# A hand-over between two stages: the first rows loaded early, the next segment's stores held, sixteen banks first

## The chip, the cores and the metric

The kernel runs on one core of a Trainium2 chip. The metric is the device time of one launch in microseconds (us). Three runs of the kernel before gave 1132.73, 1129.9 and 1131.68; their median, 1131.68, is the time before.

## What is computed

The input `x` has 64 batches of 128 channels and 2048 time steps, all in float32. Two residual layers follow each other:

```python
W = weights[condition]                       # one 128x128 matrix per batch
x = x + einsum('bct,bcd->bdt', x, W)         # layer 0
K = 2 * real(sum_n Ct[h,n] * exp(dtA[h,n] * l))   # a 2048-tap filter per channel, 64 modes
y = irfft(rfft(x, 2L) * rfft(K, 2L))[:L] + x * D  # causal convolution per channel
x = x + y * (t < length[b])                  # layer 1
```

Layer 0 mixes the channels of one batch; layer 1 filters along time within one channel, for all batches. The kernel never takes a transform: it does the convolution in blocks of 128 steps (a Toeplitz matrix inside a block, a recurrence of 64 modes from block to block).

## The kernel before, in words

Time is cut into two segments of 1024 steps (s = 0 and 1).

**The batch stage.** Layer 0 works batch by batch. `fetch(s, n)` loads two batches (1 MB) from `x` on the SP queue into a tile `xb`; `weigh` picks the batch's 128x128 matrix on GpSimd; `project` multiplies it on TensorE in banks of 512 columns, copies each bank back into `xb`, mostly on ScalarE (ACT), and stores the finished batch (512 KB) to a scratch tensor `scr[s]` in DRAM, by a transfer issued on the ACT queue. All 64 batches of segment 0 are done in this stage (`batch0`), while the filter's tables are made between them.

**The group stage.** Layer 1 works by groups of four channels. `load(i)` brings group i back from `scr` with the batches (and two halves of the segment) as 128 partitions: a tile `x` of 128 rows x 2048, 1 MB. There are 32 groups per segment, 64 iterations in all. In `iteration(i)`, for each of four channels n: `turn(i + 1, n)` transposes the next group's channel on TensorE (tile `tr`, line 831) and ACT copies it (`u`, line 832); `inputs` multiplies it (`v`, line 856) and ACT scales the product into `s` (line 861); `inside` multiplies the present group by its Toeplitz blocks (`y`, line 897); and `some` does a few banks of segment 1's layer 0 (`p`, line 459). Then VectorE runs the recurrence (`scan`), TensorE adds its part (line 909), and `store` writes the output.

**Who does segment 1's layer 0.** Its 128 banks (64 batches, two banks each) are spread over the first 28 iterations. `FILL` banks are done up front: before, `some(8)` ahead of the first iteration and 4 within it (i = -1, which only prepares group 0); the other 116 are dealt over iterations 0 to 27, so that four of these take 5 banks and the rest 4.

**What sets the order.** The order is written by hand: each engine runs its instructions in the order in which the Python code calls them. `xb` and `x` tiles share ten buffers in rotation, so a load waits until the tile ten allocations before it is stored. Transfers issued on the SP and ACT queues share eight completion semaphores, dealt out in turn over both queues; an instruction that issues a transfer first waits until the transfer that had its semaphore before has landed, and everything behind it on its engine waits with it. Within PSUM, `p` (after the batch stage), `tr` and the table tile `pb` share two buffers, so a bank or a transpose waits for ACT's copy of the one before last.

Group 0 needs rows of all 64 batches: `load(0)` is issued after the batch stage and waits for the store of batch 63.

Of the kernel before, what the change touches and what calls it, by code (L numbers as in the profile page):

```python
# [41 lines left out]
F32 = mybir.dt.float32  # L42
# [6 lines left out]
P = 128  # L49
# [322 lines left out]
def cond_resid_ssm_kernel(  # L372
# [13 lines left out]
    nc = tc.nc  # L386
    ctx.enter_context(tc.manual_schedule())
    B, C, L = x.shape
# [4 lines left out]
    HL = SL // 2  # L393
# [5 lines left out]
    NG = NP // GP  # L399
    CG = 2 * GP  # L400
# [11 lines left out]
    big = ctx.enter_context(tc.tile_pool(name="big", bufs=10))  # L412
# [4 lines left out]
    scr = [dram.tile([P, C, HL], F32, tag=f"scr{s}", name=f"scr{s}") for s in range(NS)]  # L417
# [17 lines left out]
    def fetch(s, n):  # L435

        xbs[s, n] = big.tile([P, BT, SL], F32, tag="x", name=f"xb_{s}_{n}")
        src = x[n * BT : (n + 1) * BT, :, s * SL : (s + 1) * SL]
        nc.sync.dma_start(xbs[s, n], src.rearrange("b c t -> c b t"))

    def weigh(s, b):

        w1s[s, b] = s0.tile([P, C], F32, tag="w1", name=f"w1_{s}_{b}")
        at = nc.values_load(
            ci[:, b : b + 1],
            engines=(mybir.EngineType.Pool,),
            min_val=0,
            max_val=S - 1,
            skip_runtime_bounds_check_because="it is clamped above",
        )  # L450
        nc.gpsimd.tensor_copy(w1s[s, b], wres[:, bass.ds(at, 1), :].rearrange("p s d -> p (s d)"))  # L451

    def project(s, b, q, ps, n_banks=1, copy=nc.scalar.copy):

        n, r = divmod(b, BT)
        own = xbs[s, n][:, r, :]
        for k in range(n_banks):
            cols = slice((q + k) * BK, (q + k + 1) * BK)
            nc.tensor.matmul(ps[:, k], w1s[s, b], own[:, cols], start=True, stop=True)  # L459
        cols = slice(q * BK, (q + n_banks) * BK)  # L460
        copy(own[:, cols], ps.rearrange("p k t -> p (k t)"))  # L461
        if q + n_banks == QB:
            to = scr[s].rearrange("(f b) c t -> b c f t", f=2)[b]
            nc.scalar.dma_start(to, own.rearrange("c (f t) -> c f t", f=2))
            del w1s[s, b]
            if r == BT - 1:
                del xbs[s, n]

    def batch0(b, copy=nc.scalar.copy):
        if b % BT == 0 and b // BT + AHEAD < B // BT:  # L470
            fetch(0, b // BT + AHEAD)
        if b + WAHEAD < B:
            weigh(0, b + WAHEAD)
        project(0, b, 0, psp.tile([P, QB, BK], F32, tag="y", name=f"p0_0_{b}", bufs=2), QB, copy)
# [7 lines left out]
    def exps(g):  # L482

        for i in range(TP):
            nc.scalar.activation(es[g][:, i, 0, :], steps, AF.Exp, scale=par_of(DRE, g, i))  # L485
# [137 lines left out]
    def partial_angles(k):  # L623

        own = parts[:, :, 0:NL]
        by_l = some_l.unsqueeze(1).to_broadcast([P, NP, NL])

        def of(row, n):
            return gtab[:, row, :].unsqueeze(2).to_broadcast([P, NP, n])

        if k == 0:
            V.tensor_tensor(own, of(FHI, NL), by_l, ALU.mult)
        elif k == 1:
            V.tensor_scalar(whole, own, MAGIC, MAGIC, ALU.add, ALU.subtract)
        elif k == 2:
            V.tensor_tensor(own, own, whole, ALU.subtract)
        elif k == 3:
            V.tensor_tensor(whole, of(FLO, NL), by_l, ALU.mult)
        elif k == 4:
            V.tensor_tensor(own, own, whole, ALU.add)  # L640
        else:
            V.tensor_tensor(parts[:, :, 0:8], parts[:, :, 0:8], of(PHI, 8), ALU.add)
            V.tensor_tensor(parts[:, :, 24:25], parts[:, :, 24:25], of(PHI, 1), ALU.add)
            V.tensor_scalar(last, parts[:, :, 24:25], MAGIC, MAGIC, ALU.add, ALU.subtract)
            V.tensor_tensor(last, parts[:, :, 24:25], last, ALU.subtract)
            V.tensor_scalar(dcol, dcol, 1.0, None, ALU.add)
# [66 lines left out]

    SPAN = 28
    pieces = [(s, b, q) for s in range(1, NS) for b in range(B) for q in range(QB)]
    FILL = 12
    begun = told = done = 0

    def due(i):

        return min(len(pieces), FILL + (len(pieces) - FILL) * (i + 1) // SPAN)

    def some(n):
        nonlocal done
        for s, b, q in pieces[done : done + n]:
            weights_for(done + WAHEAD * QB + 1)
            project(s, b, q, psp.tile([P, 1, BK], F32, tag="tr", name=f"p0_{s}_{b}_{q}", bufs=2))
            done += 1

    def fetches(n):  # L730

        nonlocal begun
        while begun < min(n + BT * QB, len(pieces)):
            fetch(pieces[begun][0], pieces[begun][1] // BT)
            begun += BT * QB

    def weights_for(n):
        nonlocal told
        while told < min(n, len(pieces)):
            weigh(*pieces[told][:2])  # L740
            told += QB

# [14 lines left out]
    for now in range(12, B):  # L759
        batch0(now, V.tensor_copy if now < 18 else nc.scalar.copy)  # L760
        if now == 12:
            with nc.allow_non_contiguous_dma(reason="128 gains, four times"):
                for i in range(TP):
                    nc.gpsimd.dma_start(dcol[i * NR : (i + 1) * NR, :], dbyrow.rearrange("(h r) -> r h", r=NR))
        if now < FIRST:
            partial_angles(now - 12)
        if now < 18:
            exps(2 * now - 20)
            exps(2 * now - 19)
        for lag, step in STEPS.items():  # L770
            g, odd = divmod(now - FIRST - lag, 2)
            if not odd and 0 <= g < NT:
                step(g)
        if now == 60:
            fetches(FILL)
    assert not ps and not ts and not ks
    tmp.__exit__(None, None, None)
    early.__exit__(None, None, None)


    s1 = ctx.enter_context(tc.tile_pool(name="s1", bufs=2))
    xs, us, ss, bts, tts, ys = {}, {}, {}, {}, {}, {}
    half = [slice(0, B), slice(B, P)]
    NI = NS * NG

    def seg(i):
        return divmod(i, NG)

    def load(i):
        s, g = seg(i)  # L790
        xs[i] = big.tile([P, CG, HL], F32, tag="x", name=f"x_{i}")
        nc.sync.dma_start(xs[i], scr[s][:, g * CG : (g + 1) * CG, :])

    def toeplitz(i):

# [5 lines left out]
    def input_weights(i):  # L801

        s, g = seg(i)
        bts[i] = s1.tile([P, GP, 4, N], F32, tag="bt", name=f"bt_{i}")
        if s > 0:
            nc.sync.dma_start(bts[i].rearrange("p d k m -> p (d k m)"), btd[g])
            return
        pb = psp.tile([P, GP, 4, N], F32, tag="tr", name=f"pb_{i}", bufs=2)
        for d in range(GP):
            pair = g * GP + d  # L810
            for part in range(2):
                to = pb[:, d, part : 4 - part : 3 - 2 * part, :]
                nc.tensor.transpose(to, es[pair // TP][:, pair % TP, part, 1:NE], ident)  # L813
        nc.scalar.copy(bts[i], pb)  # L814
# [117 lines left out]
    def iteration(i):  # L932

        nxt = i + 1 < NI
        if i + 2 < NI and seg(i + 2)[0] > 0:
            input_weights(i + 2)
        if i + 3 < NI:
            load(i + 3)
        fetches(due(i + 1))
        if nxt:  # L940
            toeplitz(i + 1)
            if seg(i + 1)[0] == 0:
                input_weights(i + 1)
            states(i + 1)
        quota = due(i) - done
        for n in range(CG):
            if nxt:
                turn(i + 1, n)
            if nxt and n > 0:
                inputs(i + 1, n - 1)  # L950
            if i >= 0:
                inside(i, n)
            some(quota * (n + 1) // CG - quota * n // CG)
        if i > 0:
            store(i - 1)
        if i >= 0:
            carry_on(i)
        if nxt:
            inputs(i + 1, CG - 1)
            keep_weights(i + 1)  # L960
            scan(i + 1, 0, 2 if seg(i + 1)[0] == 0 else 1)
        for d in range(GP):
            if i >= 0:
                outputs(i, d)
            if not nxt:
                store(i, d)
            if nxt and d == 0:
                scan(i + 1, 2, 3) if seg(i + 1)[0] == 0 else scan(i + 1, 1, 2)
        if nxt:
            scan(i + 1, 3 if seg(i + 1)[0] == 0 else 2, NQ)  # L970
    load(0)
    load(1)
    some(8)
    for i in range(-1, NI):
        iteration(i)

# [31 lines left out]
```

## Time and profile before

| What | us |
|---|---|
| median of 3 runs | 1131.68 |
| the profiled execution's own time | 1130.9 |
| span of that execution's trace | 1129.1 |
| TensorE busy in the span | 1078.6 |
| batch stage: last batch copied, at | 186.59 |
| first transpose of group 0, at | 200.45 |
| one iteration with 4 banks / with 5 banks | 16.56 / 17.41 |

All times within an execution count from the start of the span. A busy TensorE says that it had matmuls in flight. "Granted clock" is the share of full speed that TensorE's throttle allowed. The DMA share is the mean busy share of the core's 16 DMA engines.

### The profile page before, as it was taken

What the parts mean: (1) busy time and instruction counts of PE and PEld (TensorE: products, weight loads), DVE (VectorE), ACT (ScalarE), POOL (GpSimd) and SP (SyncE); (2) the same over time, 40 slices, a digit from 0 to 9 for tenths busy, and PEclk for the clock granted to TensorE, in tenths of its full rate; (3) what the DMA queues carried; (4) which work ended last, traced back from release to release, by engine and by line L of the source; (5) the groups of instructions that cost most, each with busy time, mean ns of one, the idle gap of its engine ahead of it and who ended that gap; (6) DMA issues with size and microseconds to landing.
All of it is one profiled execution on the core that took longest, in us unless ns stands there. A gap on an engine that the chain in (4) does not pass through costs nothing.

```text
span 1129.1 us, 23838 instructions
## 1 busy us (share of the span) xinstructions
PE 1078.6 (96%) x8634; PEld 787.5 (70%) x8634; DVE 802.5 (71%) x2671; ACT 680.1 (60%) x1123; POOL 232.5 (21%) x404
## 2 busy tenths in 40 slices
PE   5579998899999999999999999999999999999996
PEld 2224443477777777777767768888888888888885
DVE  7555660376676676667567658888888888888887
ACT  2567665656765666665666566566566556556652
POOL 2112432112212222221221211221111121121110
PEclk9889999899999999999999999999999999999999
DMA  9999999979999999999999887787777788777764
GB/s 276 414 395 369 398 411 389 396 234 309 312 293 302 281 299 309 298 281 300 310 267 297 272 242 225 239 220 217 230 233 224 216 239 228 209 243 226 214 165 117
DMA packets 117462, 313.25 MB, mean 277 GB/s; under 512 B 12002, under 2 KB 12386, under 8 KB 109154
## 3 DMA queue, kind: packets, MB, share of 16 engines
q1 hardware_dynamic: 70928, 218.65, 61.8%
q10 hardware_dynamic: 35986, 67.84, 16.1%
q0 software_dynamic: 10432, 25.25, 8.9%
q8 instruction: 68, 1.11, 0.4%
q14 instruction: 48, 0.39, 0.1%
HBM read 164.76 MB, written 146.93 MB: 276 GB/s over the span
## 4 chain that ended last, share of the span: by engine, by line
PE 90%; DVE 3%; DMA 3%; ACT 2%; issue 1%; ACTq 0%; POOLq 0%; SPq 0%; DVEq 0%; POOL 0%
PE y L909 21%; PE y L897 20%; PE v L856 18%; PE p L459 17%; PE tr L831 10%; DMA scr<-xb 2%; PE pb L813 2%; PE pt L662 1%; PE pk L692 1%; ACT xb L461 1%; DMA x<-scr 1%; DVE s L871 1%; ACT e L485 0%; DVE xb L461 0%; DVE x L918 0%
## 5 line engine op out<-in xcount | busy, mean ns | idle before, releaser
L871 DVE SCALAR_TENSOR_TENSOR s<-s,ptab 128x128 f32<-128x128 f32 x1792 | 521.4, 346 | 110.7 <-ACT s L861 94.9
L861 ACT ACTIVATE s<-v,ptab 64x512 f32<-64x512 f32 (+1 forms) x512 | 335.6, 655 | 50.8 <-PE v L856 33.9
L897 PEld LDWEIGHTS y<-tt,u 128*128 128x128 f32 x2048 | 263.6, 192 | 80.4 <-issue 66.9
L459 PE MATMUL p<-xb,w 128*128 128x512 f32 x512 | 259.1, 619 | 28.5 <-POOL w L451 13.0
L897 PE MATMUL y<-tt,u 128*128 128x128 f32 x2048 | 270.1, 275 | 0.1
L909 PEld LDWEIGHTS y<-e,s 64*128 64x128 f32 x4096 | 233.9, 188 | 46.5 <-issue 24.1
L856 PE MATMUL v<-u,bt 128*128 128x512 f32 (+1 forms) x512 | 248.6, 567 | 0.0
L909 PE MATMUL y<-e,s 64*128 64x128 f32 x4096 | 246.7, 275 | 1.4 <-DVE s L871 1.4
L832 ACT COPY u<-tr 128x512 f32<-128x512 f32 x256 | 150.4, 588 | 158.4 <-PE tr L831 131.8
L880 DVE TENSOR_SCALAR s<-s 128x128 f32<-128x128 f32 x448 | 100.4, 224 | 137.9 <-ACT s L861 137.9
L461 ACT COPY xb<-p 128x512 f32<-128x512 f32 (+1 forms) x186 | 133.2, 717 | 88.9 <-PE p L459 80.3
L918 DVE COPY_PREDICATED x<-mask,y 128x1024 f32<-128x1024 uint8 x128 | 166.7, 1303 | 1.0 <-PE y L909 1.0
L831 PE MATMUL tr<-ident,x 128*128 128x128 f32 x1024 | 156.5, 276 | 5.5 <-DMA x<-scr 5.5
L831 PEld LDWEIGHTS tr<-ident,x 128*128 128x128 f32 x1024 | 121.8, 142 | 56.4 <-issue 50.9
L459 PEld LDWEIGHTS p<-xb,w 128*128 128x128 f32 x512 | 88.2, 199 | 96.5 <-issue 69.3
L451 POOL COPY w<-wres 128x128 f32 x128 | 59.0, 462 | 315.6 <-PE p L459 305.0
L799 POOL DMA_DIRECT2D tt<-kpad x64 | 50.1, 783 | 208.9 <-DVE s L871 173.3
L856 PEld LDWEIGHTS v<-u,bt 128*128 128x128 f32 x512 | 79.9, 192 | 13.8 <-issue 13.6
L844 POOL DMA_DIRECT2D s<-carry x64 | 45.1, 709 | 128.0 <-PE y L909 118.6
L814 ACT COPY bt<-pb 128x512 f32<-128x512 f32 x32 | 18.7, 586 | 87.3 <-PE pb L813 86.5
L888 POOL DMA_DIRECT2D carry<-s x64 | 43.6, 727 | 65.9 <-DVE s L871 60.8
L841 POOL MEMSET s<- 128x384 f32 x32 | 14.5, 454 | 148.3 <-DMA carry<-s 74.2
(193 smaller groups left out, 288.5 us busy)
## 6 DMA issues: line engine op xcount, KB each, us to landing
xb<-in_x_dram SPq DMA_DIRECT2D x64, 1024.0 KB, 9.8
scr<-xb ACTq DMA_DIRECT2D x128, 512.0 KB, 8.5
x<-scr SPq DMA_DIRECT2D x64, 1024.0 KB, 8.0
out_dram<-x SPq DMA_DIRECT2D x126, 512.0 KB, 5.7
tt<-kpad POOLq DMA_DIRECT2D x64, 256.0 KB, 5.6
btd<-bt SPq DMA_DIRECT2D x32, 256.0 KB, 7.3
bt<-btd SPq DMA_DIRECT2D x32, 256.0 KB, 4.9
carry<-s POOLq DMA_DIRECT2D x64, 64.0 KB, 7.0
```

The lines of the kernel that those rows point to most:

```text
L451: nc.gpsimd.tensor_copy(w1s[s, b], wres[:, bass.ds(at, 1), :].rearrange("p s d -> p (s d)"))
L459: nc.tensor.matmul(ps[:, k], w1s[s, b], own[:, cols], start=True, stop=True)
L461: copy(own[:, cols], ps.rearrange("p k t -> p (k t)"))
L831: nc.tensor.transpose(tr[:, k, :], xs[i][:, c, k * Q : (k + 1) * Q], ident)
L832: nc.scalar.copy(u, tr)
L856: nc.tensor.matmul(v[:, 0:nv], w, us[i, n].rearrange("p k r -> p (k r)")[:, 0:nv], start=True, stop=True)
L861: nc.scalar.activation(own[:, 0:nv], v[lanes, 0:nv], AF.Copy, scale=amp)
L871: nc.vector.scalar_tensor_tensor(new[:, d, 0:2], src, factor, own[:, d, 0:2], ALU.mult, ALU.add)
L880: nc.vector.tensor_scalar(old[:, :, 2], old[:, :, 0], -1.0, None, ALU.mult)
L897: nc.tensor.matmul(y[:, k, :], u[:, k, :], tts[i][:, n, :], start=(k == 0), stop=False, skip_group_check=True)
L909: nc.tensor.matmul(ys[i, d][:, c, k, :], st[half[c], d, part, k, :, :].rearrange("p f b -> p (f b)"), e[half[c], pair % TP, part, 0:Q], st ...
L918: nc.vector.copy_predicated(xs[i][:, d::2, :].rearrange("r c (k t) -> r c k t", k=KK), keep_k.unsqueeze(1).to_broadcast([P, 2, KK, Q]), ys ...
```

## The change

It has three parts, all at the seam between the stages:

1. `FILL` goes from 12 to 16: twelve banks of segment 1 run ahead of the first iteration (`some(FILL - CG)`, with `CG` = 4) and four within it. The other 112 are then 4 in each of 28 iterations. A fifth `xb` tile of segment 1 is fetched before group 0 is loaded, because `fetches` covers `FILL` banks and one tile more.
2. `load(0)` is cut by batches: after batch 62's instructions, rows of batches 0 to 55 are loaded in two transfers (one per half of the segment, 56 rows each); after the batch stage, the rows of batches 56 to 63 in two more (8 rows each).
3. Stores of segment 1's batches go through a list `held`. In the batch stage (s = 0) a batch is stored at once, as before. From then on `release` is called once for each n of an iteration: in iteration -1 it issues one held store per call, afterwards all that are held.

```diff
+    held = []
+
+    def release(n=None):
+        for s, b, own in held[:n]:
+            to = scr[s].rearrange("(f b) c t -> b c f t", f=2)[b]
+            nc.scalar.dma_start(to, own.rearrange("c (f t) -> c f t", f=2))
+        del held[:n]
...
         if q + n_banks == QB:
-            to = scr[s].rearrange("(f b) c t -> b c f t", f=2)[b]
-            nc.scalar.dma_start(to, own.rearrange("c (f t) -> c f t", f=2))
+            held.append((s, b, own))
+            if s == 0:
+                release()
...
-    FILL = 12
+    FILL = 16
...
+    EARLY = 56
...
+    def load(i, b0=0, b1=B):
+
+        s, g = seg(i)
+        if b0 == 0:
+            xs[i] = big.tile([P, CG, HL], F32, tag="x", name=f"x_{i}")
+        own = scr[s][:, g * CG : (g + 1) * CG, :]
+        if b1 - b0 == B:
+            nc.sync.dma_start(xs[i], own)
+        else:
+            for f in (0, B):
+                nc.sync.dma_start(xs[i][f + b0 : f + b1], own[f + b0 : f + b1])
...
-        if now == 60:
+        if now == 59:
             fetches(FILL)
+        if now == 62:
+            load(0, 0, EARLY)
...
             some(quota * (n + 1) // CG - quota * n // CG)
+            release(None if i >= 0 else 1)
...
-    load(0)
+    load(0, EARLY, B)
     load(1)
-    some(8)
+    some(FILL - CG)
```

More of the change, by code (lines that the diff above doesn't have):

```diff
@@ L741, in weights_for, with seg @@
             told += QB
+    EARLY = 56
+    xs = {}
+    def seg(i):
+        return divmod(i, NG)
+    def load(i, b0=0, b1=B):
[8 more added lines that the diff above has]
+                nc.sync.dma_start(xs[i][f + b0 : f + b1], own[f + b0 : f + b1])
     ps = {}
@@ L781, in cond_resid_ssm_kernel @@
     s1 = ctx.enter_context(tc.tile_pool(name="s1", bufs=2))
-    xs, us, ss, bts, tts, ys = {}, {}, {}, {}, {}, {}
+    us, ss, bts, tts, ys = {}, {}, {}, {}, {}
     half = [slice(0, B), slice(B, P)]
     NI = NS * NG
[L786 to L792, printed above, removed]
     def toeplitz(i):
```

## The prediction

> **What bounds the kernel now.** I read the page first, then the chain of waits around the seam, then TensorE's timeline and the table of stretches there.
>
> ```profile
> PE 1078.6 (96%) x8634; PEld 787.5 (70%) x8634; DVE 802.5 (71%) x2671; ACT 680.1 (60%) x1123; POOL 232.5 (21%) x404
> PE   5579998899999999999999999999999999999996
> DMA  9999999979999999999999887787777788777764
> ```
>
> TensorE is the bound from the sixth slice on; only the first 200 us, where the DMA engines are full, have slack to give. The chain shows the seam (start, us, what):
>
> ```profile
> 186.59 1.02 ACT xb L461
> 187.62 0.02 issue
> 187.64 5.66 DMA scr<-xb
> ...
> 193.57 6.75 DMA x<-scr
> 200.32 0.14 issue
> 200.45 1.09 PE tr L831 x4
> ```
>
> Batch 63 is copied, its store lands, only then group 0's load starts, and TensorE waits for that:
>
> ```profile
> 188.77 5.70 PE L459 MATMUL p<-xb,w 128*128 128x512 f32 x12 [0.50 <-POOL w L451]
> 194.31 0.64 PE L813 MATMUL pb<-ident,e 128*128 128x128 f32 x4
> 200.45 1.09 PE L831 MATMUL tr<-ident,x 128*128 128x128 f32 x4 [5.50 <-DMA x<-scr]
> ```
>
> ```profile
> 184.00:187.00 3.00, 3.00 (x8) 1.33 (x8) 0.00 (x0) 1.59 (x3) 0.59 (x2) 1.00 1.05 404
> 196.00:199.00 3.00, 0.00 (x0) 0.00 (x0) 0.00 (x0) 0.40 (x1) 0.00 (x0) 0.70 0.98 371
> 199.00:202.00 3.00, 1.55 (x5) 1.25 (x6) 0.00 (x0) 0.42 (x1) 0.00 (x0) 0.50 1.02 332
> 202.00:205.00 3.00, 3.00 (x9) 1.69 (x8) 0.00 (x0) 1.34 (x3) 0.00 (x0) 0.66 1.02 418
> 308.85:326.26 17.41, 17.41 (x136) 12.56 (x136) 10.97 (x37) 11.02 (x18) 2.50 (x6) 1.00 0.94 294
> ```
>
> The last three columns are granted clock, DMA share and GB/s. The pause is 5.50 us and leaves TensorE at half clock for some 4 us more. But the DMA share is 1 before, in and after it: transfers, not their order alone, are short here. The last row is an iteration with five banks (17.41 us against 16.56 for four).
>
> **Part 1: four banks moved to the front.** No work is added. Four iterations of 17.41 become 16.56: 4 x 0.85 = -3.4 us. In the seam the twelve banks cost about 0.88 us each; the present rate there, 1.03, includes an ACT store issue (0.37 us) every second bank, which now is held. TensorE's fill then runs to about where the load lands (below), so it costs nothing; without that cover it would cost the 3.4 back.
>
> **Part 2: the early load, and the fifth fetch ahead of it.** In the built order the SP queue holds, after the fetch issued at 172.46 (landing took 8.4 us, so 180.8): the fifth fetch (its buffer is free when batch 53's store, issued 169.98, 9.6 us, has landed: 179.6), the two 56-row loads (after batch 55's store), then the two 8-row loads (after batch 63's). In the semaphores dealt to them lies a new wait: ACT's store of batch 60 now waits for the fifth fetch to land, that of batch 63 for the first 56-row load. That such waits hold ACT is in the trace, early in the batch stage:
>
> ```profile
> 27.58 0.37 ACTq L464 DMA_DIRECT2D scr<-xb  x1
> 27.99 1.01 ACT L461 COPY xb<-p 128x1024 f32<-128x1024 f32 x1 [2.23 <-DMA xb<-in_x_dram]
> ```
>
> When does the fifth fetch land? The last two fetches landed 177.0 and 180.8: 3.8 us for 1 MB beside stores. So 180.8 + 1.2 to start + 3.8 = 186 (at the earliest 184.6 without a start; by the plain 8.4 us, 188). Batch 60's store would be issued at 182.49; ACT waits 3.5 us (2.1 to 5.5). Behind it on ACT is the copy of batch 61, which frees the PSUM buffer of batch 63: TensorE pauses about 184.9 to 187.4. Batch 63 is copied at 190.3, stored at 190.4 instead of 187.64, after the first 56-row load (about 189).
>
> When does that store land? The last four stores before landed 1.28 us apart, 0.52 MB each, 0.41 MB/us: the DMA engines were full. The fetch and the 56-row loads put 1.05 + 0.92 = 1.97 MB ahead, 4.8 us: 193.3 + 4.8 = 198.1 (if stores were served first, 190.4 + 5.7 = 196.1; at worst 200). The two 8-row loads follow on idle engines. The nearest row is the quickest output store of 0.5 MB between 200 and 700 us: 4.4 us to landing, of which 1.3 is data at 0.41 MB/us: 3.1 us fixed. The Trainium skill (DMA: Bandwidth & Descriptors, Anatomy of one DMA) puts a transfer's fixed part at about 2.0; by it the group would be there 1.1 us sooner. I take the row: 201.3 (199 to 203). The same page (Why a DMA increments its semaphore by 16 and not by 1) speaks against the cut: a load is spread over the largest count up to 16 that divides its rows, so 56 rows use 14 engines, 8 rows use 8. No row here has such a shape; at the full 0.41 MB/us the two early loads take 2.25 us, at 14 of 16 engines 2.6. They end before batch 63's store, so I add 0; at most 0.3.
>
> TensorE: batch 63's matmuls end 189.1, the first two banks follow, the third waits for ACT (190.8 + 0.6): 191.5, ten more at 0.88: 200.3, the table transposes 0.6 and the last copy: ready at 201.1. So the first transpose starts at 201.3 instead of 200.45: +0.9. The pause before it is almost gone: full clock. The first transposes, bank and second copy now take 4.27 us to ACT's second `u` copy; at full clock 3.1: -1.2. The Trainium skill (TensorE: Matmul & The Clock Gate, Part 1) says the clock halves after an idle window of about 3.4 us; the 5.50 us pause agrees (0.50 in the row). My new pauses, 2.5 and 2.4 us, lie below it and no row has one like them: by the rule 0, if they count like the long one, up to 1.2 each. I take 0.
>
> **Part 3: held stores.** Off the path they cost nothing in the fill. In iteration -1, where ACT's own chain is the limit (copies 0.58, scalings 1.38, bank copies 0.58, issue 0.37), there is one issue more on the path: +0.5. In iteration 0 four stores are issued together after the first bank's copy (line 861's work and the next `u` copy queue behind): 1.5 us, which TensorE's own 3 us of work covers. But the fourth store's semaphore was last given to the seventh fetch of segment 1, and that fetch waits for the two first held stores. Those are issued about 203.7 and 206.6. Their landing: a store issued 207.04 took 9.9 us among big loads, giving 216.5; by bytes the SP queue (4.4 MB from 201.3 on, with 1 MB of stores) is empty at 214.7. I take 214.7, since nothing else is queued then. The fetch: 4.4 us at the least, 10.5 by the row at 215.74 which had a load ahead of it; with 1 MB of stores beside it 5.8: 220.5. ACT would want to issue at 218.15: waits 2.4 us (0 to 8.9). Behind it are the copy of `u` and so TensorE's third transpose, then all of iteration 0: +2.4. VectorE's scan of group 0 has 3.4 us to spare there. GpSimd's Toeplitz load and its memset slip behind two more weight copies (0.3 us each), needed only 7 us later; SP has three issues more, in an idle stretch.
>
> **Sum.** -3.4 + 0.9 - 1.2 + 0.5 + 2.4 = -0.8 us against the profiled execution's 1130.9 (span 1129.1 and 1.8 around it): 1130.1. That execution lies 0.8 below the median; I say 1130.5.
>
> **The rivals.**
> *A. It works as meant.* The fetch lands near 184.6, stores get more than their share, and the held ones land before the seventh fetch is wanted: group 0 is there at about 200, with the fill; no wait in iteration 0. -3.4 - 0.4 - 1.2 + 0.5 = -4.5, and -6 with the fixed part by the page: 1125 to 1127. For it: ample slack per iteration afterwards. Against: DMA share 1.05 just where 1.97 MB are put ahead of the last store. Chance 0.30.
> *B. The fourth held store's wait decides.* With the rows' 9.9 and 10.5 us the seventh fetch lands at 227: ACT waits 8.9, TensorE with it, sum +5.7: 1136.6, slower. It turns the sign from a wait of 3.2 us, and passes the measurable from about 7.4. For it: both rows lie beside the place. Against: their queues were fuller. Chance 0.16.
> *C. The early load waits for the last store anyway.* The built order gives it batches 54 and 55 alone; excluded but for contention, which is in the sum.
>
> **The numbers.** The central case (0.54) spans 1128 to 1135; a change of 0.3% (3.4 us: 1128.3 to 1135.1) is about what a measurement of this kernel can tell from none. Faster: A and 0.06 from the central case's lower edge, 0.36; slower: B and 0.04 from its upper edge, 0.20; the same 0.44. The range 1125.5 to 1136 leaves out the tails of A and B.
>
> **What would show it.** Iterations all at 16.56; ACT idle before batch 61's copy, released by a fetch; the first transpose at 200 to 203 with a pause under 2 us and clock near 1; in iteration 0 an ACT gap of 2 to 3 us after four issues. Wrong would be: no ACT wait at batch 60 (then A), the transpose after 204, or an ACT gap over 7 us (B).

## The result, and the profile after

The changed kernel took 1136.85 us (median of 7 runs, 1135.31 to 1139.47) against 1129.53 for the kernel before (7 runs beside it, 1125.03 to 1132.73): a ratio of 1.0069, with a 95% interval of 1.0044 to 1.0094. It is slower by 7.3 us, outside the range that was given. The profiled execution took 1138.36 us with a span of 1136.6, 7.5 more than before's 1129.1.

The page first: the engines' busy time, and TensorE's slices.

```profile
PE 1080.7 (95%) x8634; PEld 787.5 (69%) x8634; DVE 802.3 (71%) x2671; ACT 681.8 (60%) x1123; POOL 230.7 (20%) x404
PE   5579999699999999999999999999999999999996
```

TensorE's work is what it was; the eighth slice (199 to 227 us) fell from 8 to 6. The chain of waits through the seam (start, us, what):

```profile
176.48 8.81 DMA xb<-in_x_dram
...
185.37 0.37 ACTq L458
...
186.93 14.46 PE p L467 x28
...
202.25 0.63 PE tr L852 x4
...
206.04 11.97 DMA scr<-xb
218.08 8.09 DMA xb<-in_x_dram
226.25 0.37 ACTq L458
...
226.66 0.59 ACT u L853
...
227.30 1.11 PE tr L852 x4
```

Before, group 0's load (`x<-scr`) was in the chain; now it is gone from it, and two fetches of `xb` stand there (the fifth and the seventh tile of segment 1), each followed by an issue on ACT (`ACTq L458`, the line of the stores in `release`). This is what the two engines did there, TensorE and then ACT, from their timelines:

```profile
186.93 14.45 PE L467 MATMUL p<-xb,w 128*128 128x512 f32 x28 [2.31 <-ACT xb L469]
...
202.25 0.63 PE L852 MATMUL tr<-ident,x 128*128 128x128 f32 x4 [0.40 <-ACT xb L469]
...
227.30 1.11 PE L852 MATMUL tr<-ident,x 128*128 128x128 f32 x4 [9.06 <-ACT u L853]
```

```profile
185.78 1.01 ACT L469 COPY xb<-p 128x1024 f32<-128x1024 f32 x1 [3.54 <-DMA xb<-in_x_dram]
...
190.46 0.37 ACTq L458 DMA_DIRECT2D scr<-xb  x1
...
215.29 11.33 ACTq L458 DMA_DIRECT2D scr<-xb  x4
226.66 0.59 ACT L853 COPY u<-tr 128x512 f32<-128x512 f32 x1 [10.84 <-DMA scr<-xb]
```

The 5.50 us pause ahead of group 0's first transpose has shrunk to 0.40, and TensorE is released there by its own fill. In its place stands one of 9.06 us in iteration 0: ACT's four store issues, begun at 215.29, take 11.33 us. The first three by themselves (the fourth is in the chain above, at 226.25):

```profile
215.29 0.37 ACTq L458 DMA_DIRECT2D scr<-xb  x1
...
218.09 0.45 ACTq L458 DMA_DIRECT2D scr<-xb  x1
...
218.63 1.21 ACTq L458 DMA_DIRECT2D scr<-xb  x1
```

There are two waits. The second of the four is issued only when the second store of iteration -1 has landed (206.04 + 11.97), which stops ACT for about 2.3 us; the fourth only when the seventh fetch has landed (218.08 + 8.09), for about 6.4. ACT's label names a store; the chain shows the fetch. The stretches (TensorE's busy time after the comma; granted clock, DMA share and GB/s last):

```profile
187.00:190.00 3.00, 3.00 (x5) 1.24 (x6) 0.00 (x0) 1.59 (x2) 0.30 (x1) 0.71 1.00 296
190.00:193.00 3.00, 3.00 (x7) 1.07 (x5) 0.00 (x0) 1.60 (x3) 0.29 (x1) 0.72 1.01 367
...
208.00:217.00 9.00, 8.46 (x42) 5.09 (x40) 4.15 (x18) 6.93 (x12) 0.29 (x1) 1.00 1.02 408
...
226.00:229.00 3.00, 1.70 (x5) 1.25 (x6) 0.00 (x0) 2.30 (x4) 0.00 (x0) 0.50 1.06 434
229.00:232.00 3.00, 3.00 (x11) 2.38 (x10) 0.35 (x1) 2.08 (x4) 0.00 (x0) 0.50 1.01 404
...
299.00:315.56 16.56, 16.56 (x133) 12.19 (x132) 11.00 (x37) 10.46 (x18) 3.48 (x6) 1.00 0.98 301
```

The long pause ends at 227.30 and is followed by more than 5 us at half clock; an iteration with four banks, as all 28 now have, takes the expected 16.56 us (last row).

### The profile page after: what moved, and what is told of

The parts are those of the page before. It is cut to its first block, busy times and chain, and to the rows that moved or that the text cites. A ratio compares the mean times of both kernels' runs of the same rounds, so it can differ in the third digit from the quotient of the medians.

```text
span 1136.6 us, 23830 instructions
## 1 busy us (share of the span) xinstructions
PE 1080.7 (95%) x8634; PEld 787.5 (69%) x8634; DVE 802.3 (71%) x2671; ACT 681.8 (60%) x1123; POOL 230.7 (20%) x404
## 4 chain that ended last, share of the span: by engine, by line
PE 88%; DMA 6%; DVE 2%; ACT 2%; issue 1%; ACTq 0%; SPq 0%; DVEq 0%
PE y L930 21%; PE y L918 20%; PE v L877 18%; PE p L467 16%; PE tr L852 10%; DMA xb<-in_x_dram 3%; DMA scr<-xb 3%; PE pb L834 2%; PE pt L671 1%; ACT xb L469 1%; PE pk L701 1%; DVE s L892 1%; ACT e L494 0%; DVE xb L469 0%; ACTq L458 0%
## 5 line engine op out<-in xcount | busy, mean ns | idle before, releaser
L467 PE MATMUL p<-xb,w 128*128 128x512 f32 x512 | 260.3, 622 | 27.2 <-DMA xb<-in_x_dram 12.1
L451 POOL COPY w<-wres 128x128 f32 x128 | 55.9, 438 | 279.6 <-PE p L467 268.9
```

## The experiments

The theory after this result, **W**: the time went into the fourth held store's wait for the seventh fetch, which itself was asked for only when the second store of iteration -1 had landed. Its rivals: **X**, that the burst of four stores among full queues holds ACT, whatever the semaphores; **H**, that holding the stores is what lets group 0's rows arrive in time, so that giving it up costs as much as the wait does (**H+**: every store has to be held for that); **E**, that the early load and the fetch ahead of it cost time by themselves, since they hold ACT and put bytes ahead of the last stores; **L**, that the seam is short of transfers whatever the order, so that a wait taken away comes back elsewhere.

To compare the profiles the seam is cut in four legs: the issue of batch 56's store (ahead of all that differs), the issue of batch 63's store, the first transpose of group 0, the first output products of group 0 (`y<-e,s`), and the end of the span. All are starts in the timelines. The moment of batch 56's store itself moves between 172.8 and 180.6 us from one profiled execution to the next, for one kernel too (b3_hold4 and b3_again), so spans of single profiles are not compared, but legs are. "Sum" is the four legs against those of before (953.5 us). A leg is read from one profiled execution of each kernel, and the sums differ from the differences of the medians by up to 2.6 us (e1_no_hold: -0.2 against +2.4), which the legs do not explain.

| Kernel | 56 to 63 | 63 to transpose | transpose to outputs | outputs to end | sum | median, us | ratio to before (95%) |
|---|---|---|---|---|---|---|---|
| before | 12.0 | 12.8 | 25.5 | 903.1 | | | |
| after | 15.1 | 11.8 | 34.7 | 899.6 | +7.7 | 1136.85 | 1.0069 (1.0044 to 1.0094) |
| e4_fill16 | 12.4 | 14.7 | 26.4 | 899.7 | -0.3 | 1129.02 | 0.9994 (0.9979 to 1.0010) |
| e1_no_hold | 13.4 | 14.6 | 25.8 | 899.5 | -0.2 | 1131.80 | 1.0022 (1.0009 to 1.0035) |
| e8_no_early | 12.0 | 11.8 | 33.3 | 899.7 | +3.3 | 1134.76 | 1.0048 (1.0036 to 1.0061) |
| e3_shift | 16.9 | 11.1 | 27.8 | 899.5 | +1.8 | 1131.34 | 1.0010 (0.9995 to 1.0025) |
| e2_one_per_call | 14.2 | 12.5 | 27.6 | 901.5 | +2.3 | 1133.48 | 1.0021 (1.0001 to 1.0041) |
| e10_hold2 | 14.5 | 12.9 | 23.5 | 899.6 | -3.0 | 1129.12 | 0.9992 (0.9982 to 1.0001) |
| b3_hold4 | 12.1 | 12.4 | 24.5 | 899.7 | -4.8 | 1124.12 | 0.9963 (0.9944 to 0.9981) |
| b3_again | 11.7 | 12.3 | 24.7 | 899.8 | -5.0 | 1127.42 | 0.9976 (0.9965 to 0.9987) |
| e9_fetch_late | 13.7 | 11.1 | 27.7 | 899.6 | -1.4 | 1128.25 | 0.9989 (0.9976 to 1.0002) |
| b8_nofetch_hold2 | 12.0 | 11.2 | 28.3 | 900.5 | -1.5 | 1128.09 | 0.9981 (0.9966 to 0.9995) |
| b7_late_hold2 | 13.1 | 11.6 | 25.2 | 899.6 | -4.1 | 1126.73 | 0.9987 (0.9973 to 1.0000) |

The kernel before had medians of 1129.38 (beside e1, e3, e4, e8), 1128.92 (b3_hold4, e9, b8, b7) and 1130.25 us (e10, e2, b3_again). The fourth leg is the same gain of about 3.5 us in all but two (e2_one_per_call, whose half clock lasts beyond the first outputs, 0.50 from 235 to 238 us, and b8_nofetch_hold2, whose last 40 output products ran at half clock and took 4.13 us, against 2.50 in b7_late_hold2): part 1 of the change. All else lies in the first three.

### One part at a time

**e4_fill16**: before, with 16 banks first and nothing else.

```diff
-    FILL = 12
+    FILL = 16
-    some(8)
+    some(FILL - CG)
```

> The kernel before with sixteen banks first and nothing else (FILL 16, so also the fifth fetch ahead of group 0's load). Theory W: four banks fill part of the 5.5 us pause; the fetch ahead makes group 0 arrive 2 to 3 us later, at about 203, so a pause of 2 to 3 us is left; the time is 1 to 3 us under before (-3.4 for the banks, +2 for the later start, less half-clock time). If the fetch ahead costs as much as the banks gain, the time is the same as before.

Measured: no change, the second of the two cases named, and not W's 1 to 3 us. The 3.4 us come off the iterations that had five banks and are given back ahead of group 0, whose rows also land later: from TensorE's timeline

```profile
202.56 0.63 PE L831 MATMUL tr<-ident,x 128*128 128x128 f32 x4 [3.58 <-DMA x<-scr]
```

**e1_no_hold**: after, with every store issued at once; the early load stays.

```diff
-            if s == 0:
-                release()
+            release()
```

> The changed kernel with every store issued at once, none held; sixteen banks first and the early load stay. Theory W: no store waits for a late fetch, because the stores of the fill land early and the seventh fetch is issued early; six store issues lie in the fill and compete with group 0's last rows, so the first transpose starts at 203 to 204, and the time is 1 to 3 us under before. Theory H (holding is what lets the early load arrive): group 0 arrives at 205 or later with a pause over 2 us, and the time is at or above before.

Measured: 5.1 us under the median of after, and still 2.4 over before. H's forecast came (first transpose after 205, a pause over 2 us, a time above before), W's gain of 1 to 3 us did not. The wait in iteration 0 is gone (third leg 25.8), as W has it, but the second leg grew from 11.8 to 14.6: the first transpose is again late for its rows.

```profile
205.41 1.09 PE L851 MATMUL tr<-ident,x 128*128 128x128 f32 x4 [3.23 <-DMA x<-scr]
```

So holding has its worth: it takes about 2.9 us off the second leg, with the early load (14.6 to 11.8) or without (e4 to e8, 14.7 to 11.8).

**e8_no_early**: after without the early load.

```diff
-        if now == 62:
-            load(0, 0, EARLY)
-    load(0, EARLY, B)
+    load(0)
```

> The changed kernel without the early load: group 0 is loaded whole after the batch stage; sixteen banks first and held stores stay. In the order of the built program the fourth held store of iteration 0 again has the semaphore of the seventh fetch. Theory W: it stays slow, 5 to 8 us over before, with the same ACT gap of 7 to 10 us in iteration 0. Theory E (the early load and its place in the semaphores, which held ACT 3.5 us at batch 61, are the loss): it falls to within 2 us of before.

```profile
187.74 6.76 DMA scr<-xb
194.73 4.62 DMA x<-scr
...
203.28 11.70 DMA scr<-xb
215.04 7.73 DMA xb<-in_x_dram
...
222.84 0.37 ACTq L458
```

In this chain batch 63's store, group 0's whole load (1 MB, 4.62 us) and then the same pair of store and fetch follow each other. The first transpose comes as early after batch 63 as with the early load (11.8 us), and batch 63 is stored 3 us sooner in the first leg. So the early load brought nothing that TensorE could use: its twelve banks and table transposes end only 0.8 us sooner. The gap of iteration 0 is there without it (ACT 10.20 us, TensorE 8.41), and the median lies 5.4 us over before, as W had it (5 to 8); E, by which it would have come within 2, is not the main loss.

### The wait itself

**e3_shift**: after, with one more transfer of 4 bytes on SP behind `load(0, EARLY, B)`. It moves every semaphore dealt after it by one, and nothing else of weight.

```diff
     load(0, EARLY, B)
+    spare = big.tile([1, 1], F32, tag="spare", name="spare", bufs=1)
+    nc.sync.dma_start(spare, d_in[0:1].rearrange("(o d) -> o d", o=1))
     load(1)
```

> The changed kernel with one spare 4-byte load issued on SP between the rest of group 0's load and group 1's: it moves every later transfer's semaphore on by one, so that none of the four held stores issued together in iteration 0 has the semaphore of the seventh fetch; nothing else changes. Theory W (the fourth held store's semaphore wait, 226.25 less about 217, and the half clock after it, are the loss): ACT still waits for the landing of batch (1,0)'s second half-pair store, about 2.5 us at the same place, but no longer for the fetch; the pause of 9.1 us on TensorE falls to about 2, outputs of group 0 start near 227 instead of 237, and the time is 2 to 4 us under before (ratio 0.996 to 0.998). Theory X (the burst of four stores among full transfer queues, not the semaphore, holds ACT): the time stays 6 to 8 us over before.

```profile
218.02 2.95 ACTq L458 DMA_DIRECT2D scr<-xb  x4
```

```profile
221.65 0.93 PE L852 MATMUL tr<-ident,x 128*128 128x128 f32 x4 [2.88 <-ACT u L853]
```

The four issues (ACT's timeline, then TensorE's) now take 2.95 us instead of 11.33. The seventh fetch is still asked for at 218.02, but no store waits for it. What is left, 2.88 us on TensorE, has two parts on ACT: the first held store's wait for the second store of iteration -1 (206.57, 11.38 us), some 1.7 us, and the 2.95 us of the four issues in a row. The median lies 5.5 us under that of after, so X, which kept it 6 to 8 us over before, falls. W's gain of 2 to 4 us over before did not come either: the median is 2.0 over it, and the ratio can't be told from 1. In the legs, what stands against the gain is the first (16.9 us; ACT waited 4.60 us for the fifth fetch) and this rest.

**e2_one_per_call**: after, one held store per call in iteration 0 too.

```diff
-            release(None if i >= 0 else 1)
+            release(None if i > 0 else 1)
```

> The change with one edit: in iteration 0 too only one held store is issued per call, not all at once. The first store to wait for the seventh fetch is then asked for one or two calls later, but the fetch is still asked for only when the second store of iteration -1 has landed. Theory W: the ACT gap stays, 5 to 9 us instead of 10.84, and the time is 1 to 5 us under the change's, at 1132 to 1136, still over before. If it is the burst of four stores that costs (0.37 us each and their bytes together) and not the wait: gap under 2 us, the time under before.

```profile
211.07 11.36 DMA scr<-xb
222.51 9.25 DMA xb<-in_x_dram
...
231.83 0.37 ACTq L458
```

The chain is the same, entered later: ACT waits 5.29 us (5 to 9 expected). So the long wait does not come from issuing the stores in a burst.

**e10_hold2**: after with one edit, the first two batches of segment 1 stored at once.

```diff
-            if s == 0:
+            if s == 0 or b < 2:
```

> The change itself, early load and fifth fetch where it has them, with one edit: segment 1's first two batches are stored at once, and only the later ones are held. The semaphores are then dealt so that no held store of iteration 0 was preceded by the seventh fetch. ACT's wait ahead of batch 61's copy (3.54 us in the change) stays. Theory W (the wait for the seventh fetch is what the change lost): the ACT gap of 10.84 us in iteration 0 is gone or under 3 us, the outputs of group 0 come at 226 to 229, and the time is 6 to 11 us under the change's, at 1126 to 1130. Theory E (the early load and the fetch ahead of it hold ACT and cost 2 to 3 us by themselves): it is 2 to 4 us above b3_hold4 in the same call. Rival L (the seam is short of transfers, and a wait of the same size comes back elsewhere): over 1133.

```profile
203.31 18.61 DMA xb<-in_x_dram
```

With its two stores gone early, the seventh fetch is asked for at 203.31 and not at 218.08. It takes 18.61 us in the full queue and lands at 221.92, nearly in time: ACT waits 1.31 us for it and at most 1.42 us in iteration 0, the third leg falls from 34.7 to 23.5 us, and the median is 1.1 us under before, not told from it (0.9982 to 1.0001). L falls here: no wait of that size comes back.

### A version without the losses, and the price of the early load

**b3_hold4** and **b3_again**: as e10_hold2, but without the early load (the diff of e8_no_early and that of e10_hold2 together).

> No early load, 16 banks first, and of segment 1's stores those of its first two batches go out at once, the others are held as in the change. Only two held stores are then left for iteration 0, and none of them has a semaphore last given to a fetch that is still to land. Theory W (the change lost its time to the fourth held store's wait for the seventh fetch): no ACT gap after group 0's first `u` copies, the first transpose at 199.5 to 201.5 as in e8_no_early (199.49), the first outputs of group 0 at 222.5 to 225 against 226.06 before, and with 3.4 us from the even iterations a time 4 to 7 us under before. Rival H+ (group 0's rows need every store held, as in e1_no_hold and e4_fill16, where the first transpose came at 205.41 and 202.56): first transpose after 202, the time within 2 us of before. Rival L (whatever goes first, the transfers of the seam are short by the same bytes): a wait of 7 us or more of another kind in iteration -1 or 0, the time not under before.

> b3_hold4 once more, so that e10_hold2 is compared with it on one chip, and to see whether its ratio (0.9963, 0.9944 to 0.9981) holds: 0.994 to 0.998 expected, with the early load's price as above.

```profile
197.29 0.63 PE L850 MATMUL tr<-ident,x 128*128 128x128 f32 x4 [1.43 <-DMA x<-scr]
...
214.66 0.66 PE L850 MATMUL tr<-ident,x 128*128 128x128 f32 x4 [1.38 <-ACT u L851]
```

```profile
197.49 0.38 SPq L439 DMA_DIRECT2D xb<-in_x_dram  x1
```

TensorE's two longest pauses between batch 63 and the outputs are 1.43 and 1.38 us, and SP asks for the seventh fetch at 197.49. Measured twice, the ratio was 0.9963 and 0.9976, both intervals under 1: it beats both kernels, by 3 to 5 us against before, with two stores not held: H+ falls. Against e10_hold2, measured beside it, b3_again is 1.7 us faster in the median; the first leg differs by 2.8 (11.7 and 14.5), since e10_hold2 keeps ACT's wait for the fifth fetch (3.42 us). The two ratios' intervals touch (0.9982 to 0.9987), but the runs themselves, 13 and 16 beside each other, differ by 2.3 us in the mean, 1.3 to 3.3 when they are resampled: E's price is there in the time too, below the 2 to 4 us forecast by the median and within it by the mean.

**e9_fetch_late**, **b8_nofetch_hold2**, **b7_late_hold2**: the fifth fetch asked for behind group 0's rows. e9 is after with

```diff
         if now == 59:
-            fetches(FILL)
+            fetches(FILL - CG)
...
     load(1)
+    fetches(FILL)
```

b7 is e9 with the edit of e10_hold2, and b8 is b7 without the early load.

> The change with its fifth fetch asked for behind group 0's rows and not ahead of them; early load and held stores stay. This takes ACT's wait ahead of batch 61's copy away (3.54 us in the change), and deals the semaphores so that no held store waits for the seventh fetch; the held stores of iteration 0 can still wait for the second store of iteration -1 to land. Theory W: in iteration 0 an ACT gap of 0 to 3 us in place of 10.84, first transpose at 198 to 200, outputs of group 0 at 223 to 226, the time 2 to 6 us under before. If the early load by itself costs (as e1_no_hold against e4_fill16, +3 us, and the change against e8_no_early say), it is the worse of this call by 1 to 3 us against b8_nofetch_hold2. If the wait for the fetch was only where a shortage of transfers showed, the gap comes back at another instruction with 6 us or more, and the time is at or over before.

> No early load, the fifth fetch behind group 0's load, 16 banks first, the first two batches of segment 1 stored at once and the others held. Against b3_hold4 only the place of the fifth fetch differs (ahead of group 0's load there, behind it here). If the 1 MB of the fetch delays the last stores of the batch stage (theory: bytes ahead of batch 63's store), the first transpose comes 1 to 2.5 us sooner than in b3_hold4; but TensorE's twelve banks end only at about 199 to 200, so of this not more than 1 us shows in the time: equal to b3_hold4 within 1.5 us, 4 to 7 us under before. If the late fetch then misses the fill (its banks wait for it), TensorE pauses 1 to 3 us in iteration -1 or 0 and it is slower than b3_hold4 by that.

> As b8_nofetch_hold2, with the early load of batches 0 to 55 kept: this pair says what the early load is worth when no store waits for a fetch. Theory E (the early load only puts 0.92 MB and two more waits ahead of the last stores): first transpose 1 to 3 us later than in b8_nofetch_hold2, the time 0 to 3 us longer. Theory of the change (rows loaded early shorten the last load): first transpose 1 to 3 us sooner, the time 0 to 2 us shorter.

e9 was expected 2 to 6 us under before and is 0.7 under, within its interval. ACT's two waits, from its timeline:

```profile
211.25 1.39 ACT L882 ACTIVATE s<-v,ptab 64x512 f32<-64x512 f32 x2 [3.10 <-DMA scr<-xb]
...
214.73 3.08 ACTq L458 DMA_DIRECT2D scr<-xb  x4
217.85 0.58 ACT L853 COPY u<-tr 128x512 f32<-128x512 f32 x1 [2.60 <-DMA scr<-xb]
```

The wait for the seventh fetch is gone, and two lesser ones are there. b8, expected 4 to 7 under, is 0.8 under in the median and 2.1 by the ratio. Of its two alternatives the second has the time right, but not the reason: the fifth fetch, put last, was issued at 195.92 and landed at 207.92, ahead of the first bank of iteration 0 (214.62). ACT's issues wait again, the last of them for the seventh fetch (202.05, 21.74 us):

```profile
216.94 3.53 ACTq L458 DMA_DIRECT2D scr<-xb  x2
...
224.27 0.58 ACT L851 COPY u<-tr 128x512 f32<-128x512 f32 x1 [1.29 <-DMA xb<-in_x_dram]
```

b7 and b8 differ in the early load alone, and their ratios (0.9987 and 0.9981) can't be told apart; E had given b7 up to 3 us more. So the time shows no price of the early load there. Where the fifth fetch stands ahead of it, it cost 2.4 to 3.0 us in the first leg (after against e8, e10 against b3; 1.0 in e1 against e4, whose medians are 2.8 apart); and in no pair did it shorten the second leg (e1 and e4, after and e8, b7 and b8 within 0.4 us, e10 0.5 longer than b3). The fetch's place alone is not the cure: moved behind the rows it takes 1.4 us off the first leg and 1.3 off the second and puts 1.6 on the third (e10 and b7); without the early load it takes 1.2 off the second and puts 3.8 on the third (b3_hold4 and b8).

## Why the prediction was wrong

It went the way of rival B, given 0.16, and B's sign came, an ACT gap over 7 us (10.84); the central case was wrong above all in one term. That B's time (1136.6) was met almost to the digit is partly luck: B's two rows were off by +2.1 and -2.4 us (12.0 and 8.1 measured for 9.9 and 10.5), and B reckoned +5.7 us where the two profiled executions differ by 7.5. Point by point against the profiled execution of before:

- **Four banks out of the loop, -3.4.** Right: 16.56 us in an iteration with four banks, and 3.5 us from the first outputs to the end.
- **The last store and the fifth fetch.** Right in what came of it: the fetch was forecast to land at 186 and landed at 185.29 (by two errors that met: it was asked for at 176.48, where the buffer was thought busy until 179.6, and took 8.81 us); ACT waited 3.54 us (3.5 forecast), batch 63 was stored at 190.46 (190.4), and the loads behind it were issued at 198.65 (198.1).
- **The first transpose, +0.9.** Measured +1.8, at 202.25 instead of 201.3. TensorE's pause before batch 63's banks was 2.31 us, and its clock stood at 0.71 and 0.72 for the six us after it, worth 1.7 us of full clock. The prediction took 0, by the clock rule of the Trainium skill (TensorE: Matmul & The Clock Gate, Part 1: half speed after an idle window of about 3.4 us). The measurement decides: 2.31 us was enough here. The bound of 1.2 that stood beside the 0 was nearer.
- **Iteration -1, -1.2 + 0.5.** It took 13.80 us before, from the first transpose to the last scaling (200.45 to 214.25), and 11.14 after (202.25 to 213.39): -2.7 and not -0.7. Of it 1.7 lie ahead of ACT's first scaling (4.57 us before, 2.87 after), where before's clock is at half. The term of +0.5 for one more issue on ACT had the wrong sign: the rest took 1.0 us less. Before, ACT stood still for 0.44 us at each of its two issues there; after, its four lie beside its arithmetic (below).
- **The fourth held store, +2.4. This is the step that failed.** From the last scaling to the first outputs it was 11.8 us before and 23.7 after: +11.9. Last scaling (212.86 + 1.39 and 212.00 + 1.39) and first outputs, before and then after:

```profile
212.86 1.39 ACT L861 ACTIVATE s<-v,ptab 64x512 f32<-64x512 f32 x2 [0.44 <-PE pb L813]
226.06 3.77 PE y L909 x64
...
212.00 1.39 ACT L882 ACTIVATE s<-v,ptab 64x512 f32<-64x512 f32 x2
237.05 3.77 PE y L930 x64
```

  The mechanism was named to the instruction; the two durations were chosen wrongly. For the second store of iteration -1 the row said 9.9 us (to 216.5) and the count of bytes 214.7; the count was taken, "since nothing else is queued then". It landed at 218.0, after 12.0 us. Up to then the DMA engines were at a share of 1.02 (208 to 217): the third and fourth held stores, another 1 MB, were issued at 208.45 and 210.89 and shared with it. For the fetch 5.8 us was taken against 10.5 of the row; it took 8.1 beside the stores that had just been released. So the fourth store was issued at 226.25 instead of 220.5: ACT waited 6.4 us for the fetch and not 2.4. A second wait the prediction put at nothing: the second of the four stores itself waited for that late store, about 2.3 us. On TensorE this made the pause of 9.06 us; it ended at half clock, which lasted to 232.63, worth another 2.7 us. The prediction had no half clock after its wait.
- **The sum** of what was measured: -3.5 + 1.8 - 2.7 + 11.9 = +7.5, as the spans differ.

The experiments bear out the cause: whatever removes only this wait takes 5 to 8 us off the median of after (e3_shift by shifting the semaphores, e10_hold2 by an earlier fetch). The weighing corrected both rows downwards. The store's row needed a correction upwards (12.0 for 9.9), the fetch's a smaller one (8.1 for 10.5, not 5.8): the argument against them ("fuller queues") forgot the stores that the change itself puts there.

## What to carry to other kernels

When transfers of two queues share completion semaphores, an issue can stop its whole engine for a transfer that it has nothing to do with; so for each transfer that is put off, list which one had its semaphore before and when that lands. A store that is held back also holds back the load that reuses its buffer: count that load from the store's landing, and release first the stores whose buffers are wanted next (here two stores at once, the others held, turned +0.7% into -0.2 to -0.4% once the early load was dropped). In a stretch where the DMA engines are full, take the duration of the nearest row with everything the change adds beside it, and not the bytes of one queue.

## What was not expected of the hardware

- **Half clock comes in stretches of 3.41 us, and where a pause falls in them counts.** After 2.31 us of pause the granted clock fell (after); after 2.19 us in the same place it did not (e10_hold2). In each trace the changes of the granted clock lie on one grid of 3.41 us. Cut along it, the tables of after and then of e10_hold2 read:

```profile
184.84:188.26 3.42, 1.33 (x3) 0.68 (x4) 0.00 (x0) 2.02 (x2) 0.21 (x1) 1.00 1.08 377
188.26:191.67 3.41, 3.41 (x5) 1.33 (x4) 0.00 (x0) 1.56 (x2) 0.30 (x1) 0.50 0.99 326
...
184.01:187.42 3.41, 1.45 (x4) 0.38 (x2) 0.00 (x0) 0.92 (x1) 0.46 (x2) 1.00 1.06 414
187.42:190.84 3.42, 3.19 (x8) 1.44 (x8) 0.00 (x0) 2.11 (x3) 0.30 (x1) 1.00 1.07 320
```

  So it is in all thirteen traces between 176 and 240 us: a stretch at full clock in which TensorE was busy for 1.41 us or less was followed by one at half clock (11 of them), and one with 1.45 us or more was not. So b8_nofetch_hold2's pause of 2.14 us (at 214.62, in a stretch with 1.27 busy) brought half clock, and one of 2.24 us that fell into two stretches (e2_one_per_call, at 191.78) did not. Why the limit lies there the runs do not show. The Trainium skill (TensorE: Matmul & The Clock Gate, Part 1) calls the window free-running, and the traces agree: the grid lies elsewhere in each execution (its changes leave 0.52 us of 3.41 in after, 3.10 in e10_hold2, counted from the span's start).
- **A transfer's issue lies beside ACT's arithmetic.** In after, ACT's two scalings run from 207.62 to 209.00, and the issue of a held store lies within them:

```profile
207.62 1.38 ACT L882 ACTIVATE s<-v,ptab 64x512 f32<-64x512 f32 x2
208.45 0.37 ACTq L458 DMA_DIRECT2D scr<-xb  x1
209.02 0.59 ACT L469 COPY xb<-p 128x512 f32<-128x512 f32 x1
```

  An issue that waits for nothing costs ACT next to none of its 0.37 us; one that waits stops it whole.
- **Cutting the load saved about 1.1 us.** The two loads of 8 rows (0.13 MB together) took 3.43 us (e2_one_per_call) and 3.51 (b7_late_hold2) from the last issue to the transpose's release, the whole 1 MB load 4.62 us (e8_no_early). At the 0.41 MB/us of the prediction, seven eighths of the bytes would be 2.2 us. No one fixed part fits both: an estimate by that rate leaves 3.1 to 3.2 us for the small loads, as the prediction's row had it, and 2.1 for the whole one. The whole one is close to the 2.0 of the Trainium skill (DMA: Bandwidth & Descriptors, Anatomy of one DMA), which that section gives for transfers issued from GpSimd; these are SP's. The prediction set its row against a figure for transfers of another kind.
